# Turning image patches into token columns: 14-row sets, flattened patches and whole transposes

## The chip, the cores and the metric

The kernel runs on one core of one Trainium2 chip. The metric is the device time of one execution in microseconds (us), and the number that counts is the median over several runs. A profiled execution has a time of its own.

## The reference

Four RGB images of 224 x 224 go through a small vision tower of two layers. The change is in the first step alone, the tokenizer: each image is cut into 28 x 28 patches of 8 x 8 pixels in 3 channels, the 192 numbers of a patch are normalised, multiplied by W1, normalised again, and sent through a small network. Attention and a mixture of experts follow, twice, in layers that the change leaves alone.

```python
patches = x.reshape(b, c, hp, P, wp, P)                     # b=4, c=3, hp=wp=28, P=8
patches = jnp.transpose(patches, (0, 2, 4, 3, 5, 1))
patches = patches.reshape(b, hp * wp, P * P * c)            # 4 x 784 x 192
tokens = layernorm(patches, ln1_g, ln1_b)
tokens = tokens @ W1 + b1                                   # 192 -> 256
tokens = layernorm(tokens, ln2_g, ln2_b)
tokens = jnp.concatenate([tokens, tokens, tokens], axis=1)  # three equal copies
h1 = silu(layernorm(tokens @ Wp1 + bp1, lnp_g, lnp_b))
return h1 @ Wp2 + bp2
```

## The kernel before

The tokens are laid out so that TensorE can multiply them: the 192 numbers of a patch have to lie on partitions, one token per column, in the tile `pT`. The image comes from DRAM the other way round, so the front of the kernel turns it.

**Load.** The tile `img` holds one row of patches per partition: partition 28b + h is patch row h of image b (112 partitions, `QP`), and in it lie 24 pixel rows (3 channels x 8) of 224 pixels. Four DMAs fill it, one for each image, two from SP's queue and two from ScalarE's (L217). The weights W1 and Wp1 and the parameters ln1 and ln2 go ahead of them (L211 to L215). Half of ln2 comes through the queue of POOL (L111), as do b1 (L112), bp1 (L170) and the many small parameters in `stage` (L175). POOL also clears eight further rows of `img` (L168): one of them later takes the standard deviations, the rest are padding that brings a column of pixels to 32 numbers.

**Turns.** `turn_patches(k, c)` turns four patch columns (`PW`), k running over 7 groups of four and c over two halves of a patch. TensorE can take one column of pixels as a strided weight of 32 columns, so a half patch is four matmuls against the identity, each of which writes 32 partitions of the PSUM tile `ptp` (L339). A float32 matmul is recorded as two passes: 14 turns x 4 patches x 4 columns x 2 passes are the 448 records of L339. ScalarE then copies each `ptp` to `pT` (L343).

**Statistics.** `patch_stats` takes the mean and variance of each patch with 28 VectorE instructions straight from `img` (L435). `patch_stds` makes the deviations of all patches from them and has ScalarE write the square roots (L446) into a row of `img` beside the last pixels, so that the second-half turns bring the deviation into `pT` as a further input of the token matmul (`SROW` is its partition).

**Folding the weights.** `first_layers` is a generator that folds both normalisations and Wp1 into one matrix `Wall` (256 inputs with padding, 512 outputs). The permutation from the order of pixels in W1 to the order in `pT`, and the subtraction of the mean, are the matrix `perm` (L465 to L470). Its parts: transposes of ln1 and ln2 (L354, L357), the bias matmul (L374), W1 through `perm` (L390, L394), the bias through Wp1 (L397), then transposes of `Wall` (L404), the product with Wp1 (L412), and the last VectorE steps (L417 to L428).

**Order.** All of this stands in one block whose order on VectorE, TensorE and ScalarE is written by hand (`tc.manual_schedule`): each of these engines works through its instructions in the order of the Python code. The block starts with 16 warm-up transposes on TensorE (L479) and ends with a transpose of `stage` (L504) and its copy to `cols` (L505, called `turned`). Outside of the block, the loads of the later weights wait for the first statistics (`arrived[0]`), and the zero fill of the DRAM tables `xrows` and `yrows` (L536) waits for `turned`.

**After it.** `first_steps` multiplies 128 tokens at a time with `Wall` (L601), in 25 tiles; `pL` collects the tokens that are left over of each image (L577). `transposed` (L267) is the helper with which the rest of the kernel turns 128 x 128 blocks. Everything behind the tokenizer is the same in both versions.

Of the kernel before, what the change touches and what calls it, by code (L numbers as in the profile page):

```python
# [21 lines left out]
F32 = mybir.dt.float32  # L22
I32 = mybir.dt.int32
AF = mybir.ActivationFunctionType
ALU = mybir.AluOpType
# [9 lines left out]
NT = NI * TPI + 1  # L35
LT = NT - 1
QP = NI * HP
TOK = NI * SEQ
REP = 3
D = 256  # L40
# [28 lines left out]
def tile_vit_tower(ctx: ExitStack, tc: tile.TileContext, a: dict, out: bass.AP):  # L69
# [10 lines left out]
    def ps_tile(name):  # L80
        return psum.tile([P, 512], F32, tag="ps", name=name)
# [82 lines left out]
    nrows = sum(k for _, k, _ in plan)  # L164
    WID = HP * PATCH
    CY = CH * PATCH
    img = tokp.tile([QP, 32, WID], F32, tag="img", name="img")
    nc.gpsimd.memset(img[:, CY:, :], 0.0)  # L168
    bp1 = tokp.tile([TT, D], F32, tag="bp1", name="bp1")
    nc.gpsimd.dma_start(out=bp1, in_=a["L0_tok_bp1"].partition_broadcast(TT))  # L170
    stage = const.tile([nrows, P], F32, tag="stage", name="stage")
# [36 lines left out]
    attr = attention.enter_context(tc.tile_pool(name="attr", bufs=2, side="right"))  # L208
    front = ctx.enter_context(ExitStack())
    tokw = front.enter_context(tc.tile_pool(name="tokw", bufs=2, side="right"))  # L210
    nc.sync.dma_start(out=W1, in_=a["L0_tok_W1"].rearrange("(s p) n -> p s n", p=KP))  # L211
    nc.scalar.dma_start(out=Wp1, in_=a["L0_tok_Wp1"].rearrange("(c p) n -> p c n", p=P))
    nc.sync.dma_start(out=ln1[:1], in_=a["L0_tok_ln1_g"].unsqueeze(0))
    nc.scalar.dma_start(out=ln2[:2], in_=a["L0_tok_ln2_g"].rearrange("(r p) -> r p", p=P))
    nc.sync.dma_start(out=ln1[1:], in_=a["L0_tok_ln1_b"].unsqueeze(0))  # L215
    for b, eng in ((0, nc.sync), (3, nc.scalar), (1, nc.sync), (2, nc.scalar)):
        eng.dma_start(  # L217
            out=img[b * HP : (b + 1) * HP, :CY, :].rearrange("h (c p) w -> h c (p w)", c=CH),
            in_=a["x"][b].rearrange("c (h p) w -> h c (p w)", p=PATCH),
        )  # L220


# [109 lines left out]
    SROW = 3 * 32 + CY  # L332

    def turn_patches(k, c):
        pt = ps_tile("ptp")
        for j in range(PW):
            x0 = (k * PW + j) * PATCH + 4 * c
            for g in range(4):
                nc.tensor.matmul(  # L339
                    pt[32 * g : 32 * (g + 1), j * QP : (j + 1) * QP], img[:, :, x0 + g],  # L340
                    ident[:QP, :QP], start=True, stop=True,
                )
        nc.scalar.copy(  # L343
            pT[:, c, :, k * PW : (k + 1) * PW],
            pt[:, : PW * QP].rearrange("p (w q) -> p q w", w=PW),
        )

    def first_layers():
# [39 lines left out]
        for i in range(2):  # L388
            for half in range(2):
                nc.tensor.matmul(  # L390
                    pp[:, i, :], perm[:, half, i].rearrange("p g k -> p (g k)"),
                    W1g[:, half, :], start=(half == 0), stop=(half == 1 and i == 0),
                )
        nc.tensor.matmul(pp[:, 1, :], srow, b1, start=False, stop=True)  # L394
# [37 lines left out]

    def patch_stats(k):
        for w in range(k * PW, (k + 1) * PW):
            got = nc.vector.bn_stats(pst[:, w, :], img[:, :CY, w * PATCH : (w + 1) * PATCH])  # L435
            arrived.append(got.ins.name)

    def patch_stds(k0, k1):
        w0, n = k0 * PW, (k1 - k0) * PW
        st, v = pst[:, w0 : w0 + n], pv[:, w0 : w0 + n]  # L440
        d = tokp.tile([QP, HP], F32, tag="pd", name="pd", bufs=2)[:, :n]
# [12 lines left out]
    perm = tokp.tile([KP, 2, 2, 4, 32], F32, tag="perm", name="perm")  # L454
    srow = tokp.tile([1, P], F32, tag="srow", name="srow")
    pst = tokp.tile([QP, HP, 6], F32, tag="pst", name="pst")
    pv = tokp.tile([QP, HP], F32, tag="pv", name="pv")
    root_ = tokp.tile([1, 1], F32, tag="root", name="root")
    one_ = ones[:1]
    ENG = mybir.EngineType  # L460
# [1 line left out]
    with tc.manual_schedule(engines=by_hand):  # L462
        nc.vector.memset(srow, 0.0)
        nc.vector.memset(srow[:, SROW : SROW + 1], 1.0)
        nc.vector.memset(perm, 0.0)  # L465
        nc.vector.memset(perm[:, :, :, :, :CY], -1.0 / PD)
        by_x = ident[:KP, :KP].rearrange("p (y x c) -> p x c y", x=PATCH, c=CH)
        for half in range(2):
            for i in range(2):
                nc.vector.tensor_scalar(  # L470
                    perm[:, half, i, :, :CY].rearrange("p g (c y) -> p g c y", c=CH)[
                        :, :, :, 4 * half : 4 * (half + 1)
                    ],
                    by_x[:, 4 * i : 4 * (i + 1)], -1.0 / PD, None, ALU.add,
                )
        nc.scalar.activation(root_, one_, AF.Sqrt, bias=one_)
        warm = ps_tile("pwarm")
        for _ in range(16):
            nc.tensor.transpose(warm[:, :P], ident, ident)  # L479
# [24 lines left out]
        nc.tensor.transpose(pc[:, :nrows], stage, ident[:nrows, :nrows])  # L504
        turned = nc.vector.tensor_copy(cols, pc[:, :nrows])  # L505
# [70 lines left out]
    for c in range(2):  # L576
        nc.vector.tensor_copy(pL[:, c, :, :LEFT], left(pTf[:, c, :]))  # L577

    def pixels(c, t):
        if t == LT:  # L580
            return pL[:, c].rearrange("p b n -> p (b n)")
        n0 = t // TPI * SEQ + t % TPI * TT
        return pTf[:, c, n0 : n0 + TT]

# [6 lines left out]
    def first_steps(g):  # L591

        tiles = turns[g]
        n = len(tiles)
        y = tokp.tile([TT, GT, D], F32, tag="y", name="y", bufs=2)
        st = small.tile([TT, GT, 6], F32, tag="st", name="st")
        mv = small.tile([TT, GT, 2], F32, tag="mv", name="mv")
        for j in range(n):
            pm = ps_tile("pw1")[:TT]
            for c in range(2):  # L600
                nc.tensor.matmul(  # L601
                    pm, pixels(c, tiles[j]), Wall[:, c, :], start=(c == 0), stop=(c == 1)
                )
# [27 lines left out]
        normed[g] = xn  # L631
# [1754 lines left out]
```

## Time and profile before

| | us |
|---|---|
| median of 3 runs | 777.82 (776.65 to 778.97) |
| profiled execution, its own time | 778.21 |
| its span in the profile | 776.5 |
| images landed | 16.74 after the start of the span |
| first turn on TensorE (L339) | 16.88 |
| first token matmul (L601) | 33.13 |

The profile names engines PE (TensorE matmuls), PEld (its weight loads), DVE (VectorE), ACT (ScalarE), POOL (GpSimd) and SP. A line of a timeline gives start, length, engine, source line, instruction, tiles (written <- read), shapes and count; in square brackets stands how long the engine was idle before it and what ended that. A line of the groups gives the busy time, the mean of one in ns, and idle time before them. Matmuls are pipelined, so that the start-to-start distance and not the recorded length of one tells what it costs. The mean granted TensorE clock in the profiled execution is 0.964 of full speed.

### The profile page before, as it was taken

The numbers are of one execution on the slowest core, as the hardware profiler recorded it, in microseconds if no ns is written. First come the engines' busy times: TensorE is split into PE (matmuls) and PEld (weight loads), VectorE is DVE, ScalarE is ACT, GpSimd is POOL, SyncE is SP. The second block draws the span as 40 slices with busy tenths as digits, with TensorE's granted clock in tenths as the row PEclk, the third lists the DMA queues.
The fourth block names the chain that finished last, engine by engine and source line by source line (L and its number), as shares of the span: only waits on it lengthen the run. The fifth ranks groups of instructions, "written<-read, shape, count | busy, mean of one in ns | idle before, by whom it ended". The sixth has DMA issues, their size and how long they took to land.

```text
span 776.5 us, 10602 instructions
## 1 busy us (share of the span) xinstructions
PE 706.8 (91%) x3407; PEld 484.9 (62%) x3407; DVE 472.9 (61%) x1486; ACT 330.9 (43%) x790; POOL 125.3 (16%) x233
## 2 busy tenths in 40 slices
PE   7989899999977887888899998669999999999997
PEld 5736555566654665777788884537776775554653
DVE  5476785769996643456444767348986845444441
ACT  1465775556683641342222326325445522222221
POOL 6300000000064234400003035715000000000000
PEclk9999999999997878999999999879999999999999
DMA  6699998000012922432324352302000013323333
GB/s 167 193 425 423 426 424 341 1 1 0 1 70 77 375 102 95 130 101 69 89 89 127 104 155 72 98 24 72 12 0 1 5 27 89 91 62 96 105 111 108
DMA packets 56175, 96.24 MB, mean 124 GB/s; under 512 B 6434, under 2 KB 46088, under 8 KB 56120
## 3 DMA queue, kind: packets, MB, share of 16 engines
q1 hardware_dynamic: 49648, 79.38, 28.8%
q0 software_dynamic: 5600, 14.32, 6.1%
q10 hardware_dynamic: 872, 1.86, 0.8%
q8 instruction: 27, 0.44, 0.2%
q14 instruction: 28, 0.23, 0.1%
HBM read 30.45 MB, written 65.09 MB: 123 GB/s over the span
## 4 chain that ended last, share of the span: by engine, by line
PE 68%; DVE 17%; ACT 6%; issue 2%; another core or an unknown queue 2%; DMA 2%; DVEq 1%; ACTq 0%
PE pb L1461 12%; PE pe L276 6%; PE pyb L1479 5%; PE pqk L1927 5%; PE ps L276 4%; PE pt L267 4%; PE pkv L276 4%; PE pw L601 3%; PE pwp L287 3%; PE ps L2336 3%; DVE oT L909 3%; PE pout L2106 2%; PE pout L2111 2%; PE pukx L2026 2%
## 5 line engine op out<-in xcount | busy, mean ns | idle before, releaser
L1100 POOL DMA_INDIRECT xrows<-xn,pos x50 | 52.9, 1058 | 249.5 <-DVE nm L959 190.2
L1684 POOL DMA_INDIRECT ys<-yrows,pos x50 | 48.4, 968 | 160.3 <-DMA yrows<-yb 124.8
L1461 PE MATMUL pb<-xTb,own 128*128 128x256 f32 (+1 forms) x240 | 56.5, 381 | 8.8 <-DVE own L1437 6.3
L1467 ACT ACTIVATE hb<-pb,own 128x256 f32<-128x256 f32 (+1 forms) x74 | 33.5, 457 | 67.0 <-PE pb L1461 52.1
L1927 PE MATMUL pqk<-Wqkv,lxT 128*128 128x512 f32 x100 | 48.8, 636 | 12.8 <-ACT lxT L90 12.8
L1479 PE MATMUL pyb<-own,hb 128*128 128x256 f32 x216 | 53.2, 387 | 1.8 <-ACT hb L1467 1.0
L1461 PEld LDWEIGHTS pb<-xTb,own 128*128 128x128 f32 x240 | 42.8, 200 | 17.4 <-ACT hb L1467 6.9
L1461 PE MATMUL pb<-hb,own 128*128 128x256 f32 (+1 forms) x240 | 52.4, 360 | 1.3 <-issue 0.7
L1485 DVE TENSOR_TENSOR yb<-pyb,eb 128x512 f32<-128x512 f32 (+1 forms) x30 | 19.1, 637 | 44.9 <-PE pyb L1479 33.7
L1479 PEld LDWEIGHTS pyb<-own,hb 128*128 128x128 f32 x216 | 41.0, 194 | 8.5 <-ACT hb L1467 1.8
L276 PE MATMUL pe<-xT,eW 128*128 128x512 f32 (+1 forms) x112 | 46.0, 553 | 0.0
L1461 PEld LDWEIGHTS pb<-hb,own 128*128 128x128 f32 x240 | 40.5, 191 | 6.5 <-issue 1.9
L601 PE MATMUL pw<-Wall,pT 128*128 128x512 f32 x96 | 42.6, 593 | 0.0
L267 PE MATMUL pt<-ident,xn 128*128 128x128 f32 x200 | 31.9, 292 | 11.4 <-DVE xn L627 6.6
L1450 ACT COPY xTb<-ptb 128x512 f32<-128x512 f32 (+1 forms) x30 | 16.2, 540 | 58.8 <-PE ptb L1446 48.5
L267 PEld LDWEIGHTS pt<-ident,xn 128*128 128x128 f32 x200 | 24.9, 148 | 26.3 <-issue 8.2
L1927 PEld LDWEIGHTS pqk<-Wqkv,lxT 128*128 128x128 f32 x100 | 19.9, 206 | 34.2 <-issue 18.8
L1469 DVE TENSOR_SCALAR hb<-pb,own 128x256 f32<-128x256 f32 (+1 forms) x46 | 20.5, 445 | 29.6 <-PE pb L1461 19.8
L863 DVE SCALAR_TENSOR_TENSOR prod<-kq 128x784 f32<-128x784 f32 x32 | 30.5, 970 | 6.1 <-ACT kq L1277 3.4
L276 PEld LDWEIGHTS pe<-xT,eW 128*128 128x128 f32 x112 | 20.2, 190 | 21.6 <-issue 16.5
L1437 DVE COPY own<-ew 128x1540 f32 x30 | 28.8, 962 | 6.3 <-ACT xTb L1450 1.9
L1941 ACT ACTIVATE qk<-qk 128x256 f32<-128x256 f32 x50 | 20.4, 408 | 25.1 <-DVE qk L1933 22.3
(418 smaller groups left out, 1466.2 us busy)
## 6 DMA issues: line engine op xcount, KB each, us to landing
xrows<-nothing SPq DMA_DIRECT2D x22, 896.0 KB
yrows<-nothing SPq DMA_DIRECT2D x22, 896.0 KB
out_dram<-h SPq DMA_DIRECT2D x23, 384.0 KB
xb<-xrows SPq DMA_DIRECT2D x24, 256.0 KB
yrows<-yb SPq DMA_DIRECT2D x24, 256.0 KB
ew<-in_L_ffn_expert_w_dram SPq DMA_DIRECT2D x6, 768.0 KB
wb<-wd SPq DMA_DIRECT2D x16, 128.0 KB
img<-in_x_dram SPq DMA_DIRECT2D x2, 588.0 KB
```

Of the source, the lines that this page charges most:

```text
L267: nc.tensor.transpose(pt[:, j * TT : (j + 1) * TT], xn[:, j, c * P : (c + 1) * P], ident[:TT, :TT])
L276: nc.tensor.matmul(pm[: wcols.stop - wcols.start, :n], w[:, c, wcols], xT(c), start=(c == 0), stop=(c == chunks - 1),)
L287: nc.tensor.matmul(pm[:, i, :], xT(c, t), w[:, c, :], start=(c == 0), stop=(c == chunks - 1))
L601: nc.tensor.matmul(pm, pixels(c, tiles[j]), Wall[:, c, :], start=(c == 0), stop=(c == 1))
L863: nc.vector.scalar_tensor_tensor(prod, qTs[s][:, o, :], 1.0, kT[:, o, t * SEQ : (t + 1) * SEQ], ALU.mult, ALU.mult, accum_out=atts[s][:, o ...
L1100: put = nc.gpsimd.indirect_dma_start(out=xrows[:, :], out_offset=bass.IndirectOffsetOnAxis(ap=pos[:, k, t0 + j : t0 + j + 1], axis=0), in_ ...
L1437: nc.vector.tensor_copy(w, ewf[0][:, bass.ds(off, EW)])
L1461: nc.tensor.matmul(pm, wm[:, c, o * P : (o + 1) * P], src[:, c, :], start=(c == 0), stop=(c == 1),)
L1467: nc.scalar.activation(dst[:, o, :], pm, AF.Relu, bias=b)
L1479: nc.tensor.matmul(pm[:, t, :], src[:, c, t * P : (t + 1) * P], wm[:, c, :], start=(c == 0), stop=(c == 1),)
L1684: got = nc.gpsimd.indirect_dma_start(out=y[:, j, k, :], out_offset=None, in_=yrows[:, :], in_offset=bass.IndirectOffsetOnAxis(ap=pos[:, k, ...
L1927: nc.tensor.matmul(pqk, xTs[u][:, c, cut(j, 1)], Wqkv[:, c, : 2 * D], start=(c == 0), stop=(c == 1),)
```

## The change

The images are loaded in sets of 14 patch rows, half an image each. Set o goes to partitions o, o + 9, o + 18, ..., so that eight sets fill places 0 to 7 of each nine; a ninth transfer reads set 0 again into place 8, whose results are not used. That makes 126 partitions (`IP`) and nine DMAs, five on SP's queue and four on ScalarE's, and the small parameters go ahead of W1 and Wp1.

A new step `flatten` copies four patches so that a patch's 192 numbers lie side by side, followed by one place for the deviation; the copies live in `flat`, which borrows the space of the later tile `vT`. Two of the seven run on VectorE and five on ScalarE. `turn_patches` then transposes a patch of all 126 rows whole, in two chunks of 128 and 65 columns: 14 turns x 4 patches = 56 transposes. ScalarE's copy out of PSUM puts rows and sets in order and drops the ninth; the last one goes to VectorE. The padding of `img` and its memset go, the warm-up is 6 transposes instead of 16, `perm` is built in one step per half, and the order written by hand is new. `K1` holds the two chunk heights for the matmuls that read `pT`.

```diff
+HH = HP // 2
+SETS = 2 * NI
+PITCH = SETS + 1
+IP = HH * PITCH
...
-    img = tokp.tile([QP, 32, WID], F32, tag="img", name="img")
-    nc.gpsimd.memset(img[:, CY:, :], 0.0)
+    img = tokp.tile([IP, CY, WID], F32, tag="img", name="img")
...
-    nc.sync.dma_start(out=W1, in_=a["L0_tok_W1"].rearrange("(s p) n -> p s n", p=KP))
-    nc.scalar.dma_start(out=Wp1, in_=a["L0_tok_Wp1"].rearrange("(c p) n -> p c n", p=P))
     nc.sync.dma_start(out=ln1[:1], in_=a["L0_tok_ln1_g"].unsqueeze(0))
     nc.scalar.dma_start(out=ln2[:2], in_=a["L0_tok_ln2_g"].rearrange("(r p) -> r p", p=P))
     nc.sync.dma_start(out=ln1[1:], in_=a["L0_tok_ln1_b"].unsqueeze(0))
-    for b, eng in ((0, nc.sync), (3, nc.scalar), (1, nc.sync), (2, nc.scalar)):
-        eng.dma_start(
-            out=img[b * HP : (b + 1) * HP, :CY, :].rearrange("h (c p) w -> h c (p w)", c=CH),
-            in_=a["x"][b].rearrange("c (h p) w -> h c (p w)", p=PATCH),
+    nc.sync.dma_start(out=W1, in_=a["L0_tok_W1"].rearrange("(s p) n -> p s n", p=KP))
+    nc.scalar.dma_start(out=Wp1, in_=a["L0_tok_Wp1"].rearrange("(c p) n -> p c n", p=P))
+    for o in range(PITCH):
+        b, i = divmod(o % SETS, 2)
+        (nc.scalar if o % 2 else nc.sync).dma_start(
+            out=img[o::PITCH].rearrange("h (c p) w -> h c (p w)", c=CH),
+            in_=a["x"][b].rearrange("c (i h p) w -> i h c (p w)", i=2, p=PATCH)[i],
         )
...
+    SROW = PD - P
+    K1 = (P, SROW + 1)
+    NPX = PD + 1
+    flat = vT.rearrange("p c n -> p (c n)")[:IP, : HP * NPX].rearrange("q (w f) -> q w f", f=NPX)
+
+    def flatten(k, put):
+        put(
+            flat[:, k * PW : (k + 1) * PW, :PD].rearrange("q w (y x) -> q w y x", x=PATCH),
+            img[:, :, k * PW * PATCH : (k + 1) * PW * PATCH].rearrange(
+                "q y (w x) -> q w y x", x=PATCH
+            ),
+        )
+
+    def turn_patches(k, c, put=nc.scalar.copy):
+        pt, n = ps_tile("ptp"), K1[c]
         for j in range(PW):
-            x0 = (k * PW + j) * PATCH + 4 * c
-            for g in range(4):
-                nc.tensor.matmul(
-                    pt[32 * g : 32 * (g + 1), j * QP : (j + 1) * QP], img[:, :, x0 + g],
-                    ident[:QP, :QP], start=True, stop=True,
-                )
-        nc.scalar.copy(
-            pT[:, c, :, k * PW : (k + 1) * PW],
-            pt[:, : PW * QP].rearrange("p (w q) -> p q w", w=PW),
+            nc.tensor.transpose(
+                pt[:n, j * IP : (j + 1) * IP], flat[:, k * PW + j, c * P : c * P + n],
+                ident[:IP, :IP],
+            )
+        put(
+            pT[:n, c, :, k * PW : (k + 1) * PW].rearrange("p (o h) w -> p o h w", o=SETS),
+            pt[:n, : PW * IP].rearrange("p (w h o) -> p o h w", w=PW, h=HH)[:, :SETS],
         )
...
         nc.scalar.activation(
-            img[:, CY, w0 * PATCH : (w0 + n) * PATCH].rearrange("q (w x) -> q w x", x=PATCH)[
-                :, :, PATCH - 1
-            ],
-            v, AF.Sqrt, bias=eps[:QP], scale=1.0 / PD,
+            flat[:, w0 : w0 + n, PD], v, AF.Sqrt, bias=eps[:IP], scale=1.0 / PD,
         )
...
-        for _ in range(16):
+        for _ in range(6):
             nc.tensor.transpose(warm[:, :P], ident, ident)
         steps = first_layers()
         next(steps)
         NK = HP // PW
         cut0 = 5
-        for k in range(3):
-            turn_patches(k, 0)
-        for k in range(cut0):
+        flatten(0, nc.vector.tensor_copy)
+        flatten(1, nc.scalar.copy)
+        turn_patches(0, 0)
+        for k in range(2):
             patch_stats(k)
+        flatten(3, nc.vector.tensor_copy)
+        flatten(2, nc.scalar.copy)
+        turn_patches(1, 0)
         next(steps)
-        for k in range(3, cut0):
-            turn_patches(k, 0)
+        for k in range(2, cut0):
+            patch_stats(k)
+        turn_patches(2, 0)
+        flatten(4, nc.scalar.copy)
         next(steps)
-        for k in range(cut0, NK):
-            turn_patches(k, 0)
+        turn_patches(3, 0)
+        flatten(5, nc.scalar.copy)
+        turn_patches(4, 0)
         patch_stds(0, cut0)
+        turn_patches(5, 0)
+        flatten(6, nc.scalar.copy)
+        for k in range(2):
+            turn_patches(k, 1)
+        turn_patches(6, 0)
         for k in range(cut0, NK):
             patch_stats(k)
-        for k in range(cut0 - 1):
+        for k in range(2, cut0):
             turn_patches(k, 1)
         patch_stds(cut0, NK)
-        for k in range(cut0 - 1, NK):
-            turn_patches(k, 1)
         next(steps)
+        turn_patches(5, 1)
+        turn_patches(6, 1, nc.vector.tensor_copy)
```

More of the change, by code (lines that the diff above doesn't have):

```diff
@@ L331, in tile_vit_tower @@
     nc.gpsimd.memset(pL, 1.0)
-    SROW = 3 * 32 + CY
-    def turn_patches(k, c):
-        pt = ps_tile("ptp")
-        for j in range(PW):
-            x0 = (k * PW + j) * PATCH + 4 * c
-            for g in range(4):
-                nc.tensor.matmul(
-                    pt[32 * g : 32 * (g + 1), j * QP : (j + 1) * QP], img[:, :, x0 + g],
-                    ident[:QP, :QP], start=True, stop=True,
-                )
-        nc.scalar.copy(
-            pT[:, c, :, k * PW : (k + 1) * PW],
-            pt[:, : PW * QP].rearrange("p (w q) -> p q w", w=PW),
+    SROW = PD - P
[11 more added lines that the diff above has]
+        pt, n = ps_tile("ptp"), K1[c]
+        for j in range(PW):
+            nc.tensor.transpose(
[5 more added lines that the diff above has]
+            pt[:n, : PW * IP].rearrange("p (w h o) -> p o h w", w=PW, h=HH)[:, :SETS],
         )
@@ L390, in first_layers @@
                 nc.tensor.matmul(
-                    pp[:, i, :], perm[:, half, i].rearrange("p g k -> p (g k)"),
+                    pp[:, i, :], perm[:, half, i * P : (i + 1) * P],
                     W1g[:, half, :], start=(half == 0), stop=(half == 1 and i == 0),
@@ L434, in patch_stats @@
         for w in range(k * PW, (k + 1) * PW):
-            got = nc.vector.bn_stats(pst[:, w, :], img[:, :CY, w * PATCH : (w + 1) * PATCH])
+            got = nc.vector.bn_stats(pst[:, w, :], img[:, :, w * PATCH : (w + 1) * PATCH])
             arrived.append(got.ins.name)
@@ L440, in patch_stds @@
         st, v = pst[:, w0 : w0 + n], pv[:, w0 : w0 + n]
-        d = tokp.tile([QP, HP], F32, tag="pd", name="pd", bufs=2)[:, :n]
+        d = tokp.tile([IP, HP], F32, tag="pd", name="pd", bufs=2)[:, :n]
         nc.vector.tensor_tensor(d, st[:, :, 1], st[:, :, 4], ALU.subtract)
@@ L446, in patch_stds @@
         nc.scalar.activation(
-            img[:, CY, w0 * PATCH : (w0 + n) * PATCH].rearrange("q (w x) -> q w x", x=PATCH)[
-                :, :, PATCH - 1
-            ],
-            v, AF.Sqrt, bias=eps[:QP], scale=1.0 / PD,
+            flat[:, w0 : w0 + n, PD], v, AF.Sqrt, bias=eps[:IP], scale=1.0 / PD,
         )
     Wall = tokp.tile([P, 2, 2 * D], F32, tag="Wall", name="Wall")
-    perm = tokp.tile([KP, 2, 2, 4, 32], F32, tag="perm", name="perm")
+    perm = tokp.tile([KP, 2, 2 * P], F32, tag="perm", name="perm")
     srow = tokp.tile([1, P], F32, tag="srow", name="srow")
-    pst = tokp.tile([QP, HP, 6], F32, tag="pst", name="pst")
-    pv = tokp.tile([QP, HP], F32, tag="pv", name="pv")
+    pst = tokp.tile([IP, HP, 6], F32, tag="pst", name="pst")
+    pv = tokp.tile([IP, HP], F32, tag="pv", name="pv")
     root_ = tokp.tile([1, 1], F32, tag="root", name="root")
@@ L465, in tile_vit_tower @@
         nc.vector.memset(perm, 0.0)
-        nc.vector.memset(perm[:, :, :, :, :CY], -1.0 / PD)
-        by_x = ident[:KP, :KP].rearrange("p (y x c) -> p x c y", x=PATCH, c=CH)
+        nc.vector.memset(perm[:, :, :PD], -1.0 / PD)
+        by_y = ident[:KP, :KP].rearrange("p (y x c) -> p c y x", x=PATCH, c=CH)
         for half in range(2):
[L469 to L475, printed above, removed]
+            nc.vector.tensor_scalar(
+                perm[:, half, :PD].rearrange("p (c y x) -> p c y x", c=CH, x=PATCH)[
+                    :, :, 4 * half : 4 * (half + 1)
+                ],
+                by_y, -1.0 / PD, None, ALU.add,
+            )
         nc.scalar.activation(root_, one_, AF.Sqrt, bias=one_)
         warm = ps_tile("pwarm")
-        for _ in range(16):
+        for _ in range(6):
             nc.tensor.transpose(warm[:, :P], ident, ident)
@@ L575, in tile_vit_tower @@
     pTf = pT.rearrange("p c q w -> p c (q w)")
-    for c in range(2):
-        nc.vector.tensor_copy(pL[:, c, :, :LEFT], left(pTf[:, c, :]))
+    for c, n in enumerate(K1):
+        nc.vector.tensor_copy(pL[:n, c, :, :LEFT], left(pTf[:n, c, :]))
     def pixels(c, t):
         if t == LT:
-            return pL[:, c].rearrange("p b n -> p (b n)")
+            return pL[: K1[c], c].rearrange("p b n -> p (b n)")
         n0 = t // TPI * SEQ + t % TPI * TT
-        return pTf[:, c, n0 : n0 + TT]
+        return pTf[: K1[c], c, n0 : n0 + TT]
     def first_rows(g):
@@ L601, in first_steps @@
                 nc.tensor.matmul(
-                    pm, pixels(c, tiles[j]), Wall[:, c, :], start=(c == 0), stop=(c == 1)
+                    pm, pixels(c, tiles[j]), Wall[: K1[c], c, :], start=(c == 0), stop=(c == 1)
                 )
```

## The prediction

> **What bounds the kernel now.** First the busy shares on the page: TensorE works in 91% of the span, so a microsecond comes off the end only if TensorE's own stream gets shorter or starts earlier.
>
> ```profile
> PE 706.8 (91%) x3407; PEld 484.9 (62%) x3407; DVE 472.9 (61%) x1486; ACT 330.9 (43%) x790; POOL 125.3 (16%) x233
> ```
>
> Next the chain that ended last, cut to the first 90 us (start, length, what):
>
> ```profile
> 2.31 14.44 DMA img<-in_x_dram
> 16.74 0.14 issue
> 16.88 3.04 PE ptp L339 x96
> ...
> 20.50 1.74 PE ptp L339 x64
> ...
> 24.16 1.77 PE ptp L339 x58
> ...
> 26.76 4.09 PE ptp L339 x160
> ...
> 33.01 0.19 PE pc L504
> 33.20 7.08 PE pw L601 x16
> ```
>
> The end hangs on the image load until 16.74, then on the 448 passes of turn_patches until 33.01; at 33.20 the token matmuls (L601) start, and from there the chain is almost all TensorE and its feeders. Their start is what I forecast: every microsecond it moves should reach the end, since the next late thing, the zero fill of xrows and yrows, is released by `turned`, just after L504, and moves along; the weights wait for the first bn_stats, which moves too.
>
> Third, the timeline of that stretch (start, length, engine, instruction, [idle before]):
>
> ```profile
> 2.59 3.67 PE L479 MATMUL pwarm<-ident 128*128 128x128 f32 x16 [2.59 <-POOL ident masks.py:199]
> 7.10 0.26 PE L357 MATMUL pgb<-ident,ln 4*128 4x4 f32 x1 [0.59 <-DMA ln<-in_L_tok_ln_b_dram]
> 14.27 2.07 PE L397 MATMUL pbw<-Wp,bb 128*128 128x256 f32 x4
> 71.41 1.04 PE L267 MATMUL pt<-ident,xn 128*128 128x128 f32 x8
> 28.55 0.54 ACT L343 COPY pT<-ptp 128x448 f32<-128x448 f32 x1 [0.23 <-PE ptp L339]
> 16.86 5.31 DVE L435 BATCH_NORM_STATS2 pst<-img 112x6 f32<-112x192 f32 x20 [1.79 <-DMA img<-in_x_dram]
> ```
>
> TensorE has a second string beside the images: folding the weights (first_layers) ends at 14.27 + 2.07 = 16.34, only 0.4 us ahead of the images. So earlier images alone buy 0.4 us on TensorE. That string starts at 7.10, when ln2's second half lands, a tiny POOL transfer issued at 1.39. ScalarE idles 0.23 us before each copy: TensorE sets the pace, one turn per 0.77 us.
>
> Last, the load's rate, from the busy time by stretches (last columns: granted clock, DMA share, GB/s):
>
> ```profile
> 10.00:12.00 2.00, 2.00 (x6) 1.64 (x5) 1.70 (x8) 0.00 (x0) 0.60 (x2) 1.00 0.89 234
> 38.00:40.00 2.00, 2.00 (x6) 0.90 (x5) 0.61 (x2) 0.37 (x1) 0.00 (x0) 1.00 0.98 412
> ```
>
> The DMA engines are about as busy during the images as in the zero fill, and move little more than half as much.
>
> [...] transposes take 3.67 / 16 = 0.23 us at first and 1.04 / 8 = 0.13 us at 71 us, and the clock column falls to 0.50 at 58.9 us after an idle 2.8 us. [...]
>
> **The change, step by step.**
>
> *Load.* W1 and Wp1 go behind three tiny loads, about 0.6 us later; their 0.45 MB then ends near 4.1 us. Nine image transfers move 9 x 14 x 3 x 7168 B = 2.71 MB instead of 2.41 (one set is read twice). Now 2.41 MB takes from 3.5 to 15.5, and landing shows 1.3 us later. At best 14 engines run at the zero fill's 412 / 16 = 25.8 GB/s each, 361 GB/s: 7.5 us. I take 7.8, so images at 4.1 + 7.8 + 1.3 = 13.2. The other bound, today's rate: 4.1 + 13 + 1.3 = 18.4, worse than now. Issues go from 4 to 9, 5 on SP and 4 on ACT, at 0.33 to 0.47 us; both queues are otherwise empty until the images land, so they are hidden, even if one waits for a semaphore as SP now does for 2.1 us. The vanished 1.60 us POOL memset of img frees `live`, for which VectorE waited until 6.5.
>
> *Weight folding.* Ten warm-up transposes go: 10 x 0.23 = 2.3 us, free only if TensorE then has ln2. I put its landing at 5.2 instead of 7.1[...]; bounds 4.4 and 7.1. The rest of the string, 9.2 us at half clock, is unchanged: it ends at 14.4 and Wall is copied by 13.1. The perm build is shorter on VectorE, well ahead of its use.
>
> *Turns.* 448 passes, 3.04 + 1.74 + 1.77 + 4.09 + 1.19 + 0.80 = 12.6 us on the chain, become 56 transposes: 7.3 us at 0.13, 12.9 at 0.23.[...]
>
> *Flattens, new.* Seven copies of 126 x 768. ScalarE copies take 0.37 us for 256 elements (L604) and 0.59 for 512 (L988), so 0.80 for 768; the bound above comes from the first row here (VectorE's from the second):
>
> ```profile
> L902 ACT ACTIVATE oT<-vT,att 128x784 f32<-128x784 f32 x5 | 4.5, 944 | 0.0
> L1437 DVE COPY own<-ew 128x1540 f32 x30 | 28.8, 962 | 6.3 <-ACT xTb L1450 1.9
> ```
>
> VectorE: 0.56[...]. Five on ScalarE are 4.0 us, two on VectorE 1.1. No flatten existed before; each stands ahead of its turn.
>
> *ScalarE becomes the pace.* 13 copies at 0.52 (0.54 alone, less overlap when back to back) = 6.8, one moved to VectorE; four of its flattens after the first copy 3.2; WcT 0.6; two square roots 0.6: 11.2 us from its first copy. That comes at 14.4 + 0.92 (four transposes at half clock) + 0.2 = 15.5. I laid the three engines' lists side by side with these durations. ScalarE then loses 2.2 us: waiting for the first turns at half clock, for the Wp1 matmuls (L412, 2.0 us of TensorE between turns 2 and 3), and for VectorE's square-root input. So its last copy ends at 28.9. The token matmuls' first half needs no second-chunk copy, as now, so they start at about 29.0; turn 6's copy on VectorE ends at 29.7, inside the 0.9 us that the first half takes. VectorE: 28 bn_stats at 0.266 = 7.4, two flattens, 1.1 of deviations, 2.0 for Wall, from 13.3: done at 24.9, hidden.
>
> *Sum.* 33.2 - 29.0 = 4.2 us, of which I take off 0.3 for semaphore hand-offs on the longer list: 3.9. The profiled execution took 778.21 (span 776.5), so 774.3; it lies 0.4 above the median of 777.82, so 773.9 to 774.3. I say **774.2**.
>
> **Rivals.**
> 1. *One of the two strings does not move.* If ln2 still lands at 7.1, folding ends at 16.3 and the same lists give 30.9: 2.3 us gained, 775.7. If the images come at 16.7, 31.8: 1.4 us, 776.6; even at 17.5, 32.2. For: the POOL landing is inferred, and reading one set twice costs bytes.[...]
> 2. *Slower: TensorE stays at half clock.*[...] All 56 transposes and the Wp1 matmuls cost double (12.9 + 3.8 us), TensorE is the bound again and L601 starts at 34.0[...]. By the lists a full clock from 21.2 on still gives 30.9, from 30 on 33.2, as now; any later is slower. For: now the clock rises only near 18 us. Against: the clock also rose at 260.3 after 2.5 us of nothing but transposes and 1 us of matmuls, so transposes count, and at half clock TensorE would be nearly always busy.
> 3. *More gain.* Full clock from 14.4, flattens at 0.75, folding done at 13.0: L601 at 27.2, 6 us, 771.8.
> 4. *The relayout is dear.* Both flatten bounds and 0.56 per copy: L601 at 29.8, 775.0; a POOL write that holds a VectorE flatten adds up to its 1.63 us (L532): 776.7.
>
> **How the numbers follow.** A measurement of this kernel tells about 0.3% (2.3 us) from no change, so faster means below 775.5. Forecast as worked: 0.46, faster. Rival 1: 0.24, of which 0.06 faster and 0.18 within the bound. Rival 3: 0.08, faster. Rival 4: 0.12, half each way. Rival 2: 0.10, slower. Faster 0.46 + 0.06 + 0.08 + 0.06 = 0.66, same 0.18 + 0.06 = 0.24, slower 0.10. The range 771.5 to 777.6 holds all but rival 2 and the tails of 1, 3 and 4.
>
> **What would show it.** Right: images landing near 13; folding's L397 ending near 14.4; transposes at 0.13 each once warm; ScalarE's idle time inside the turns gone; L601 starting at 28.5 to 30. Wrong: flattens above 1 us, L397 still ending after 16, transposes at 0.23 beyond 22 us, or an L601 that starts earlier while the end doesn't move.

## The result, and the profile after

| | before | after |
|---|---|---|
| median of 20 runs each, same chip, us | 778.12 | 773.25 |
| ratio of after to before | | 0.994 (0.9914 to 0.9965) |
| profiled execution, us; its span | 778.21; 776.5 | 774.73; 773.0 |
| images landed, us | 16.74 | 16.35 |
| folding's last bias matmul ended (L397, now L410) | 16.34 | 14.74 |
| first token matmul (L601, now L622) | 33.13 | 30.87 |

The kernel is 4.9 us faster by the medians; the forecast was 774.2. The landed time was forecast at 13.2 and the first token matmul at 29.0 to 29.3, so the sum came out close while two of its terms did not. In the fences below the lines have the numbers of the kernel after: L352 is the transposes, L342 the flattens, L356 ScalarE's copies, L425 the Wp1 matmuls, L622 the token matmuls.

TensorE's row of the busy times is as heavy a share as before, with 402 instructions fewer:

```profile
PE 702.5 (91%) x3005; PEld 479.4 (62%) x3005; DVE 475.7 (62%) x1487; ACT 333.9 (43%) x794; POOL 126.2 (16%) x232
```

The chain that ended last, first 40 us (start, length, what):

```profile
1.88 6.29 DMA img<-in_x_dram
8.18 8.17 DMA img<-in_x_dram
16.66 0.62 DVE vT L342
17.33 1.94 PE ptp L352 x8
...
20.97 2.13 PE pw L425 x8
...
23.57 0.53 ACT pT L356
24.10 0.74 ACT vT L342
...
26.84 2.06 ACT pT L356 x5
...
30.94 7.09 PE pw L622 x16
```

The chain now has two image entries: an early transfer holds the queue until 8.18, and the last transfer, issued then, lands at 8.18 + 8.17 = 16.35. In place of 448 passes on TensorE stand a flatten, a few transposes, and from 23.57 mostly ScalarE.

The timeline of the same stretch shows what TensorE and ScalarE wait for (start, length, engine, instruction, [idle before]):

```profile
5.27 0.26 PE L370 MATMUL pgb<-ident,ln 4*128 4x4 f32 x1 [0.88 <-DMA ln<-in_L_tok_ln_b_dram]
12.66 2.08 PE L410 MATMUL pbw<-Wp,bb 128*128 128x256 f32 x4
17.33 1.94 PE L352 MATMUL ptp<-ident,vT 126*128 126x126 f32 x8 [2.60 <-DVE vT L342]
20.80 2.30 PE L425 MATMUL pw<-W,WcT 128*128 128x256 f32 x8
22.94 1.02 PE L352 MATMUL ptp<-ident,vT 126*128 126x126 f32 x8
23.57 0.53 ACT L356 COPY pT<-ptp 128x448 f32<-128x448 f32 x1 [1.30 <-PE ptp L352]
```

ln2 is there at 5.27 and folding ends at 12.66 + 2.08 = 14.74, close to the forecast. But the images are not, and TensorE stands idle for 2.60 us. It comes back at half clock: eight transposes take 1.94 us (0.24 each), where eight at 22.94 take 1.02 (0.13). The clock column of the stretches stays at 1.00 there, so half clock is read from these durations, and stands below for such doubled ones. The Wp1 matmuls, partly at half clock too, stand ahead of turn 3 on TensorE, and ScalarE waits 1.30 us for that turn.

The load itself, from the busy time by stretches (length; busy us and instructions of PE, PEld, DVE, ACT, POOL; granted clock, DMA share, GB/s):

```profile
10.00:12.00 2.00, 2.00 (x5) 1.17 (x5) 0.00 (x0) 0.00 (x0) 0.00 (x0) 1.00 0.90 280
```

And the waits of SP's queue (us in total, times, longest), which issues five of the nine transfers and stops twice between them:

```profile
SPq L221 <- DMA Wp<-in_L_tok_Wp_dram: 1.2, 1, 1.2
SPq L221 <- DMA img<-in_x_dram: 1.1, 1, 1.1
```

The new layout does raise the rate, from 234 to 280 GB/s, with the engines as busy as before (0.90 against 0.89). That is 19.4 GB/s for each of 0.90 x 16 engines, not 25.8.

### The profile page after: what moved, and what is told of

It reads as the page before. It is cut to its first block, busy times and chain, and to the rows that moved or that the text cites. A ratio compares the mean times of both kernels' runs of the same rounds, so it can differ in the third digit from the quotient of the medians.

```text
span 773.0 us, 9815 instructions
## 1 busy us (share of the span) xinstructions
PE 702.5 (91%) x3005; PEld 479.4 (62%) x3005; DVE 475.7 (62%) x1487; ACT 333.9 (43%) x794; POOL 126.2 (16%) x232
## 4 chain that ended last, share of the span: by engine, by line
PE 68%; DVE 17%; ACT 7%; issue 4%; DMA 2%; DVEq 1%; another core or an unknown queue 1%; ACTq 0%
PE pb L1482 11%; PE pe L280 6%; PE pyb L1500 5%; PE ps L280 4%; PE pqk L1948 4%; PE pkv L280 4%; PE pt L271 4%; PE pw L622 3%; PE ps L2357 3%; PE pwp L291 3%; PE pukx L2047 3%; PE pout L2127 3%; DVE oT L930 3%; PE pout L2132 3%; DMA img<-in_x_dram 2%
## 5 line engine op out<-in xcount | busy, mean ns | idle before, releaser
L622 PE MATMUL pw<-Wall,pT 128*128 128x512 f32 (+1 forms) x96 | 42.7, 593 | 0.0
L1948 PEld LDWEIGHTS pqk<-Wqkv,lxT 128*128 128x128 f32 x100 | 19.9, 207 | 28.6 <-issue 26.8
L280 PEld LDWEIGHTS pe<-xT,eW 128*128 128x128 f32 x112 | 20.2, 190 | 21.6 <-issue 16.5
L1458 DVE COPY own<-ew 128x1540 f32 x30 | 28.9, 965 | 7.0 <-issue 2.6
L622 PEld LDWEIGHTS pw<-Wall,pT 128*128 128x128 f32 (+1 forms) x96 | 17.9, 189 | 20.0 <-issue 17.9
```

Of the source, the lines that this page charges most:

```text
L280: nc.tensor.matmul(pm[: wcols.stop - wcols.start, :n], w[:, c, wcols], xT(c), start=(c == 0), stop=(c == chunks - 1),)
L622: nc.tensor.matmul(pm, pixels(c, tiles[j]), Wall[: K1[c], c, :], start=(c == 0), stop=(c == 1))
L1458: nc.vector.tensor_copy(w, ewf[0][:, bass.ds(off, EW)])
L1948: nc.tensor.matmul(pqk, xTs[u][:, c, cut(j, 1)], Wqkv[:, c, : 2 * D], start=(c == 0), stop=(c == 1),)
```

## The experiments

The theory after the result: the image load still bounds the start, the shorter turns bring most of the gain, and half clock and the place of the Wp1 matmuls cost what is missing. Against it stand: the gain comes from the order of loads and the earlier folding; or from the layout of the load alone. Three sets of four ran on three chips. Before took 749.94 us in the first, 749.46 in the second and 777.47 in the third, so ratios are compared, and times inside the first 35 us, which agree between the chips (folding ends at 14.71 to 14.77 in every profile in which POOL's loads, the flattens and the 6 warm-ups are as in the kernel after and the rows lie in sets). Before itself has only the one profile above.

Two times are told for each kernel that flattens: when ScalarE's first flatten starts, which is when the images are there, and how long it is from that to the first token matmul. In the kernel after they are 16.60 and 14.27 us.

### Old transfers with the new turns

The kernel after with before's four transfers of 28 neighbouring rows.

```diff
-IP = HH * PITCH
+IP = QP
...
-            out=img[o::PITCH].rearrange("h (c p) w -> h c (p w)", c=CH),
+            out=img[b * HP : (b + 1) * HP].rearrange("h (c p) w -> h c (p w)", c=CH),
...
```

> The changed kernel with the image load of before: four transfers of 28 rows on adjacent partitions, everything else as changed. Theory A (the partitions that a transfer reaches set its rate): the load goes back to about 200 GB/s, 4.4 + 2.41 MB / 0.2 + 1.3, so the images land at 17.5 to 18 us instead of 16.35, and the token matmuls start at about 32.0 instead of 30.87; ratio to before about 0.998. Theory B (some other limit, the same for both layouts, about 280 GB/s): with 2.41 MB instead of 2.71 the images land at 14.5 to 15.3, and the token matmuls start at 29.5 to 30; ratio about 0.993.

Ratio 0.9955 (0.9927 to 0.9984). Images at 17.30, token matmuls at 32.17, 14.87 later: these times are close to Theory A's, the ratio is not (it had about 0.998). In before it is 16.27 us from the first use of the images (16.86) to the token matmuls. So the new turns are 1.4 us shorter without the new load, and the token matmuls start 0.96 us earlier although the images come late. The ratio stands for 3.4 us; what is more than the 0.96 doesn't show in the front.

### The sets alone

Before with the nine transfers and 126 rows; order of loads, warm-up and 448 passes unchanged.

```diff
-    for b, eng in ((0, nc.sync), (3, nc.scalar), (1, nc.sync), (2, nc.scalar)):
...
+    for o in range(PITCH):
...
+            out=img[o::PITCH, :CY, :].rearrange("h (c p) w -> h c (p w)", c=CH),
...
```

> The kernel before with only the nine image transfers in sets of 14 rows; its load order, 16 warm-ups, 448 passes and memset stay. Theory A: the images land earlier than 16.74, at 15.5 to 16.3. As folding the weights ends at 16.3 in any case, the turns start at most 0.4 us earlier, and with 126 rows for 112 the passes get up to an eighth longer: the token matmuls start between 32.7 and 34.3, so the ratio lies between 0.9995 and 1.0015: the sets alone bring nothing. Theory C (the earlier images are what brought the gain): they start near 31, ratio 0.997.

Ratio 0.998 (0.997 to 0.9989). The timeline of TensorE:

```profile
2.59 3.52 PE L484 MATMUL pwarm<-ident 128*128 128x128 f32 x16 [2.59 <-POOL ident masks.py:199]
...
10.80 1.13 PE L402 MATMUL pbw<-Wp,bb 128*128 128x256 f32 x4
15.48 4.51 PE L344 MATMUL ptp<-ident,img 126*32 126x126 f32 x96 [3.55 <-DMA img<-in_x_dram]
...
33.75 2.84 PE L606 MATMUL pw<-Wall,pT 128*128 128x512 f32 x6
```

The first turn starts 1.4 us earlier than in before, but after 3.55 us of idling its first 96 passes take 4.51 us where they took 3.04, and all passes are a little longer with 126 rows than with 112 (the next 64 take 1.99 us, 1.80 in before). The token matmuls start no earlier: the earlier images are spent again inside the old turns.

Two things were not expected. Folding ended at 10.80 + 1.13 = 11.93, not at 16.3: TensorE came to its full clock with the last warm-ups (16 in 3.52 us, where the same 16 took 3.67 in before), and the four bias matmuls took 1.13 us instead of 2.07. And the ratio is below 1, clear of its interval, although the token matmuls start 0.6 us later than in before. That gain of 1.5 us lies somewhere behind the front.

### Eight apart instead of nine

The kernel after with 112 partitions 8 apart and no ninth transfer.

```diff
-PITCH = SETS + 1
+PITCH = SETS
```

> The changed kernel with the sets on partitions 8 apart instead of 9: eight transfers, 112 partitions, no set read twice.[...] Theory A[...]: about 200 to 220 GB/s, so the images land at 16.7 to 17.7 us although there is 0.30 MB less to move; the token matmuls start at 31.2 to 32.2. Theory B[...]: 280 GB/s, images at 14.5 to 15.3, the token matmuls at 29.5 to 30, ratio about 0.992.

Ratio 0.999 (0.9977 to 1.0003); images at 19.13, token matmuls at 33.24, both later than either theory had them. The stretch 10 to 12 us of this kernel, then of the one with old rows:

```profile
10.00:12.00 2.00, 2.00 (x5) 1.17 (x4) 0.00 (x0) 0.00 (x0) 0.00 (x0) 1.00 0.84 195
```

```profile
10.00:12.00 2.00, 2.00 (x5) 1.00 (x3) 0.87 (x5) 0.00 (x0) 0.51 (x1) 1.00 0.92 232
```

Fewer bytes than with nine apart, and 195 instead of 280 GB/s: the rate goes with the partitions that the rows go to, and going nine apart is worth the bytes of the ninth, useless set. Being spread is not enough: 8 apart loads more slowly than side by side, 195 against 232. Why the three layouts come in this order isn't shown.

### Warmth before the first turn

```diff
         next(steps)
+        again = ps_tile("pwarm2")
+        for _ in range(10):
+            nc.tensor.transpose(again[:, :P], ident, ident)
         NK = HP // PW
```

> The changed kernel with ten more transposes of the identity on TensorE between the folding of the weights (ends at 14.7) and the first turn (17.3), where it sits idle 2.6 us. They are to end before the images are there. Theory D (the half clock until 21.7 costs time because the first turns and the Wp1 matmuls stand ahead of everything): the turns run at 0.13 us per transpose from 17.3 or soon after, and the token matmuls start at 29.7 to 30.2 instead of 30.87; ratio about 0.992 against 0.994. Theory E (ScalarE paces the turns anyway): they start at 30.5 to 30.9, no gain. The image load is the same as in the changed kernel and tells how much its landing (16.35) varies from run to run.

Ratio 0.9946 (0.9925 to 0.9967). Images at 16.42, then 13.82 us to the token matmuls at 30.24: 0.45 less than in the kernel after, and between the ranges of D and E. The first eight transposes take 1.57 us there, neither the 1.94 of half clock nor the 1.02 of full: part of them is still at half clock.

### The kernel after, again

No edit; it ran beside the next three.

> The changed kernel itself, once more, to stand beside the next three on one chip. If the front decides, its token matmuls start again near 30.9 us and its ratio to before is 0.994 to 0.996; the images land between 16.1 and 16.4 again.

Ratio 0.9959 (0.9947 to 0.9972). Images at 15.71, 0.9 us earlier than in the first profile of the same kernel and than expected, and 14.22 us to the token matmuls at 29.93, as there. The turn is steady; the landing is not.

### W1 and Wp1 first again

```diff
+    nc.sync.dma_start(out=W1, in_=a["L0_tok_W1"].rearrange("(s p) n -> p s n", p=KP))
+    nc.scalar.dma_start(out=Wp1, in_=a["L0_tok_Wp1"].rearrange("(c p) n -> p c n", p=P))
     nc.sync.dma_start(out=ln1[:1], in_=a["L0_tok_ln1_g"].unsqueeze(0))
```

> The changed kernel with W1 and Wp1 issued ahead of the three small loads again, as before the change. Theory F (the new order leaves the DMA engines without work for 0.6 us at the start, and the images bound the front, not the folding): the images land near 15.2 to 15.5 instead of 16.2, the folding ends near 15.6 instead of 14.7, the turns start near 16.2 and the token matmuls at 29.6 to 30.2: about 0.8 us less than the changed kernel, ratio lower by 0.001. Theory G (the small loads first help, since the folding starts earlier): the token matmuls start later than 30.9, or at the same time.

Ratio 0.9958 (0.9943 to 0.9974). Images at 16.95 and folding still done at 14.72: no gain. The idea that the later first packet costs 0.8 us fell.

### Wp1 matmuls behind turn 4

```diff
         turn_patches(2, 0)
         flatten(4, nc.scalar.copy)
-        next(steps)
         turn_patches(3, 0)
         flatten(5, nc.scalar.copy)
         turn_patches(4, 0)
+        next(steps)
+        flatten(6, nc.scalar.copy)
         patch_stds(0, cut0)
         turn_patches(5, 0)
-        flatten(6, nc.scalar.copy)
```

> The changed kernel with the matmuls with Wp1 (the third step of first_layers) moved behind the turns 3 and 4 in TensorE's order, and the square roots behind flatten 6 on ScalarE. Theory H (ScalarE loses 1.3 us waiting for turn 3, which stands behind these matmuls): that wait goes, the token matmuls start at 30.0 to 30.5. Theory I (the wait only moves: turn 5 then stands behind the matmuls, and the first square roots wait for a VectorE that the third flatten, 2.0 us beside POOL's writes, makes late): no gain, 30.7 to 31.

Ratio 0.9939 (0.9915 to 0.9963). From the timeline:

```profile
21.92 0.83 ACT L342 COPY vT<-img 126x768 f32<-126x768 f32 x1
22.66 0.54 ACT L356 COPY pT<-ptp 128x448 f32<-128x448 f32 x1
23.08 0.84 ACT L342 COPY vT<-img 126x768 f32<-126x768 f32 x1
23.30 1.89 PE L425 MATMUL pw<-W,WcT 128*128 128x256 f32 x8
```

Turn 3's copy (22.66) follows the flatten ahead of it with no idle time, where the kernel after waited 1.30 us. From the first flatten to the token matmuls are 13.08 us: 1.2 less. The wait was on the path, and the order by itself removes it.

### Three edits together

W1 and Wp1 first, Wp1 matmuls later, and flatten 3 in another form on VectorE.

```diff
...
-        flatten(3, nc.vector.tensor_copy)
+        flatten(3, lambda d, s: nc.vector.tensor_tensor(d, s, s, ALU.max))
...
```

> Three edits at once on the changed kernel: W1 and Wp1 first, the Wp1 matmuls behind turn 4, and flatten 3 as a maximum of a tile with itself[...]. Flatten 3 should take 0.9 to 1.0 us whatever POOL does, against 1.1 to 2.0 as a copy. If the three add up, the token matmuls start at 28.6 to 29.3 and the ratio is 0.991 to 0.993; if ScalarE is the floor whatever stands ahead of it, at 29.6 or later.

Ratio 0.9944 (0.9921 to 0.9967). Images at 17.71, 13.08 us to the token matmuls at 30.79, not 28.6 to 29.3: the same span as with the later Wp1 matmuls alone. Flatten 3 took 0.94 us here, 2.02 in the kernel after, and 0.55 to 2.16 in the other kernels that copy it; none of the difference reaches the token matmuls here.

### The order of loads and warm-up alone

Before with the small loads first and 6 warm-ups.

```diff
...
-        for _ in range(16):
+        for _ in range(6):
```

> The kernel before with only the order of the first loads and the number of warm-up transposes changed (three small loads ahead of W1 and Wp1, 6 warm-ups for 16); image rows, transfers and the 448 passes as before. Prediction's theory (the images bound the front, folding is next to them): folding ends near 14.4 to 15 instead of 16.3, but the images still land at 16.5 to 17.5, so the token matmuls start at 33.0 to 34 and the ratio to before is 0.999 to 1.002. Rival (folding is what holds the front, and the new image layout contributes little): token matmuls at 31 to 32, ratio 0.997 or less.

Ratio 1.0006 (0.9982 to 1.003). From the timeline of TensorE:

```profile
12.89 2.07 PE L397 MATMUL pbw<-Wp,bb 128*128 128x256 f32 x4
16.88 3.98 PE L339 MATMUL ptp<-ident,img 112*32 112x112 f32 x96 [1.92 <-DMA img<-in_x_dram]
...
33.70 2.84 PE L601 MATMUL pw<-Wall,pT 128*128 128x512 f32 x6
```

Folding ends at 14.96, 1.4 us earlier, and TensorE only waits 1.92 us for the images, after which its first 96 passes take 3.98 us, not 3.04. The rival that folding holds the front is out.

### Parameters behind the images

The kernel after with POOL's loads of bp1 and `stage` put into the list that waits for the first statistics.

```diff
-    nc.gpsimd.dma_start(out=bp1, in_=a["L0_tok_bp1"].partition_broadcast(TT))
...
-        nc.gpsimd.dma_start(out=stage[r0 : r0 + n, :width], in_=src)
...
+    weight_loads.append(
+        nc.gpsimd.dma_start(out=bp1, in_=a["L0_tok_bp1"].partition_broadcast(TT))
+    )
...
+        weight_loads.append(nc.gpsimd.dma_start(out=stage[r0 : r0 + n, :width], in_=src))
```

> The kernel after with POOL's loads of bp1 and of the thirteen parameter strings of stage moved behind the first bn_stats, so that nothing small shares the DMA engines with the images from about 5 us on. Theory J (small POOL packets share the engines with the image packets and hold the last of them): the stretch 6 to 12 us moves 320 GB/s or more and the images land by 15, about 1.3 us earlier than in the kernel after; token matmuls near 29, ratio to before 0.993 to 0.994. Theory K (14 partitions apart by 9 give 280 GB/s by themselves, or the issuing queues set it): 270 to 290 GB/s still, landing 15.7 to 17 as in the runs so far, ratio as the kernel after, 0.994 to 0.997.

Ratio 0.9956 (0.9931 to 0.9981). Images at 15.78, inside K's range. The 319 and 337 GB/s from 8 to 12 us are J's, the 272 from 6 to 8 are not; the last experiment decides between them. Two side effects tell more. First, POOL, no longer busy issuing, clears `nothing` early, and the timeline of POOL and VectorE shows:

```profile
5.21 1.60 POOL L555 MEMSET nothing<- 128x1792 f32 x1
...
5.59 1.47 DVE L574 TENSOR_SCALAR spare<-spare,dead 128x2 f32<-128x2 f32 x1
```

In the kernel after the same VectorE step takes 0.25 us; here it ends at 7.06, 0.25 us after POOL's write (6.81), and folding behind it ends at 16.41 instead of 14.74. The kernel of the last experiment repeats both lines, 1.60 us from 5.21 and 1.47 us from 5.59. That the write held the step is the author's reading of these times.

Second, the token matmuls start at 29.69, 1.2 us earlier than in the kernel after, but their second group of 16 starts at 62.19 against 61.98. The gain was given back in between. Stretches of the kernel after, then of this one:

```profile
54.00:56.00 2.00, 0.16 (x1) 0.18 (x1) 1.48 (x9) 1.97 (x4) 0.00 (x0) 0.90 1.06 444
...
58.00:60.00 2.00, 2.00 (x8) 1.63 (x8) 2.00 (x10) 1.98 (x3) 0.00 (x0) 0.75 1.03 434
```

```profile
54.00:56.00 2.00, 1.35 (x6) 1.13 (x7) 1.93 (x8) 1.32 (x2) 0.00 (x0) 0.50 1.01 423
...
58.00:60.00 2.00, 2.00 (x7) 1.55 (x6) 0.93 (x5) 1.19 (x2) 0.00 (x0) 0.50 0.99 416
```

The granted clock stays at 0.50 from 54 to 60 us, a longer dip, and the chain has 5.44 us for the 16 second matmuls of the tokens (L286 here) that took 4.05 (L291).

### New order and warmth together

The later Wp1 matmuls and the ten transposes in one kernel.

> The kernel after with the Wp1 matmuls behind turn 4 and flatten 6 ahead of the square roots, and ten more transposes of the identity between folding and the first turn. If the two gains are separate (the wait of ScalarE for turn 3 of 1.3 us, and turns at half clock until 21.7): 12.3 to 12.8 us from ScalarE's first flatten to the token matmuls, where the kernel after took 14.2 and each edit alone 13.1 and 13.8; ratio 0.992 to 0.994. If ScalarE's own work (11.2 us and its first flatten) is all that is left once its wait is gone, the warm-up adds nothing: 13.0 to 13.2, ratio 0.9935 to 0.995.

Ratio 0.9923 (0.9901 to 0.9945), median 771.45 beside 777.47. From the timeline of TensorE:

```profile
14.56 2.34 PE L493 MATMUL pwarm<-ident 128*128 128x128 f32 x10
17.36 1.67 PE L352 MATMUL ptp<-ident,vT 126*128 126x126 f32 x8 [0.46 <-DVE vT L342]
...
29.52 5.43 PE L625 MATMUL pw<-Wall,pT 128*128 128x512 f32 x12
```

The images come at 16.68, no earlier than in the kernel after, and 12.84 us later the token matmuls start: 1.2 us from the order, 0.2 more from the warmth, so less than two separate gains would give. Before is beaten clear of noise. Against the kernel after, the token matmuls start 1.35 us earlier, but the ratios leave it open: the kernel after had 0.994 (0.9914 to 0.9965) and 0.9959 (0.9947 to 0.9972), on other chips.

### All of it

The last two experiments in one kernel.

> The last two together: parameter loads behind the images, Wp1 matmuls later, ten transposes before the first turn. If Theory J holds: images by 15, token matmuls near 27.5 to 28, ratio 0.990 to 0.992. If Theory K holds: the same as the kernel with the new order and warm-up alone, ratio within 0.001 of it.

Ratio 0.9916 (0.9886 to 0.9947): not to be told from 0.9923. Images at 16.66. The stretch 10 to 12 us, of the kernel with parameters later and of this one, whose loads up to there are the same:

```profile
10.00:12.00 2.00, 2.00 (x6) 1.58 (x5) 1.38 (x8) 0.00 (x0) 0.52 (x3) 1.00 0.92 337
```

```profile
10.00:12.00 2.00, 2.00 (x6) 1.57 (x5) 1.40 (x8) 0.00 (x0) 0.53 (x3) 1.00 0.89 251
```

337 in one execution and 251 in the other, images at 15.78 and 16.66: POOL's small loads don't explain the landing. With them it was 15.71, 16.42, 16.60, 16.68 and 17.14. The packet records of these five traces show where the spread arises: nine tenths of the images' 7 KB packets had ended by 13.71 to 14.35 us, the last one at 14.95, 15.68, 15.68, 15.97 and 16.43, in the same order. In all ten profiles of sets 9 apart the last six packets are those of SP's queue, which has five of the nine transfers. Why they lag stays open; no kernel here shares the transfers out differently.

## Why the prediction was right, and where it was wrong

**The load** is the step that failed: "At best 14 engines run at the zero fill's 412 / 16 = 25.8 GB/s each, 361 GB/s". The 14 can be read from before's packet records: from 6 to 13 us mostly 14 image packets were under way at once, in the zero fill 16. The engines were as busy as assumed, but moved 19.4 GB/s each. In the packet records a 7 KB packet of the zero fill took 0.272 us; those of the images, from 6 to 13 us, took 0.335 on average, where they took 0.437 in before and 0.508 with sets 8 apart. They ran from 4.13 to 15.68, 11.6 us instead of 7.8: nine tenths had ended by 13.78, the last came singly. The landing showed 0.7 us after the last one, not 1.3: 16.35 instead of 13.2. SP's queue from 15 to 15.8 us (packets, MB, share of 16 engines):

```profile
q1 hardware_dynamic: 3, 0.01, 4.6%
```

Rows sent 9 apart are better than neighbouring ones (with the small loads first, flattens started at 17.30 in one execution with old rows, and at 15.71 to 17.14 in five with the sets), but their packets take longer than the zero fill's. That image packets would move at the zero fill's pace in the new layout was the author's estimate; no row of before showed it. The bound at today's rate should have been 18.9 instead of 18.4, since at 2.41 MB in 12 us the 2.71 MB take 13.5 us, not 13. The issues, costed as hidden at 0.33 to 0.47 us, took 3.52 / 4 = 0.88 each on ScalarE's queue, and SP's were spread until 8.99; whether that delays the landing wasn't separated.

```profile
1.88 3.52 ACTq L221 DMA_DIRECT2D img<-in_x_dram  x4
```

**Folding**: ln2 at 5.2 and the end at 14.4 were forecast, 5.27 and 14.74 measured. The 5.2 was the author's estimate, and why ln2 came 1.8 us earlier isn't shown. Right, and worth nothing by itself, as the prediction said of the one string without the other and the kernel with only the new order shows.

**The clock**: half was expected for the first turns only, with TensorE going from folding straight into them; when full would come was the author's estimate. With the images late it idled 2.60 us and ran at half clock until about 21.6 (two records of the Wp1 matmuls in each 0.4 us before, three and four after). Where it did go straight on, with the parameters later (turns at 16.46 behind a folding that ended at 16.41), the first eight transposes took 1.94 us as well, and the Wp1 matmuls at 19.93 were at full clock (eight in 1.99 us, as in before). Rival 2 was built on half clock, but it did not last so long that TensorE became the bound; the warmth is worth 0.45 us on its own and 0.2 beside the new order.

**ScalarE's pace** was right in kind and somewhat too slow in size. The forecast had 13.4 us from its first copy to the end of its last (15.5 to 28.9), 11.2 of work and 2.2 of waits. Measured are 12.4 (18.47 to 30.89): 10.1 of work and 0.25 + 1.30 + 0.73 = 2.3 of waits, the longest one for the turn behind the Wp1 matmuls. Flattens cost 0.83 and, back to back, 0.73 to 0.74 (0.80 assumed); copies back to back 2.68 / 6 = 0.45 (0.52 assumed). VectorE's second flatten, then the last lines of ScalarE:

```profile
19.27 2.02 DVE L342 COPY vT<-img 126x768 f32<-126x768 f32 x1
...
26.73 2.68 ACT L356 COPY pT<-ptp 65x448 f32<-65x448 f32 x6
29.30 0.33 ACT L459 ACTIVATE vT<-pv,eps 126x8 f32<-126x8 f32 x1
30.36 0.53 ACT L356 COPY pT<-ptp 65x448 f32<-65x448 f32 x1 [0.73 <-PE ptp L352]
```

The VectorE flattens cost 0.61 (0.56 assumed, an estimate of the author's) in the first and 2.02 in the second. The POOL write that Rival 4 named had ended at 19.05, and POOL went on with many small ones; where its clearing was done early, with the parameters later, this flatten took 0.55 and 0.56. So a flatten was slowed as in Rival 4, and that POOL's writes did it is the author's reading of these times; but it had time to spare. The one hand-off from the landing (16.35) to the first flatten (16.66) took as much as the whole term of 0.3 us.

**The sum.** What happened is nearest to Rival 1, images that don't move; its 31.8 for images at 16.7 was too late, in part because of ScalarE's pace. The token matmuls began 2.26 us earlier in the first pair of profiles and 3.2 in the repetition, instead of 3.9. The prediction had 3.5 of its 4.2 us from the load and 0.7 from the turns; the pair shows 0.4 from the load and 1.9 from the turns.

**From there to the end** the prediction let the gain through unchanged. The spans show 1.24 us more gained behind the first token matmul (743.37 to 742.13), 0.47 of it up to the second group (31.51 to 31.04). It isn't explained, and single executions can't explain it: on the third chip, where before takes about as long as here (777.47), the four profiles have 735.6 to 744.6 from the first token matmul to the end, over the same instructions. Part of that spread is the clock dip near 56 us, which took 1.4 us back where parameters came later. The old rows and the sets alone show the same gap: by the ratio they gain 2.4 and 2.1 us more than the start of their token matmuls does, against the one profile of before. So 774.2 met 773.25 with a front 1.6 us short, and with 1.24 us behind it and a median that moved 4.9 us where the profiled pair moved 3.5. None of that was in the forecast, and that the number was met so closely is luck.

## What to carry to other kernels

A transfer's rate is to be taken from a row with the same shape of packets and partitions, not from the fastest row of the page: rows nine partitions apart raised 234 to 280 GB/s, not to 361. A load is there only with its slowest packets: nine tenths of this one had ended 1.9 us before the last. When one of two strings into a stage is shortened, work out what the engine does in the gap: here it idled 2.60 us, and ten transposes put there were worth 0.45 us. And where an in-order engine feeds the engine that sets the pace, moving a block that nobody needs yet (eight matmuls, 2 us) behind the next feeds was worth 1.2 us, half of what the first pair of profiles shows for the whole front.

## What the runs showed of the hardware that was not expected

- Image transfers with rows 9 apart took 0.88 us each to issue on ScalarE's queue (and so did rows 8 apart), against 0.44 for rows side by side in before.
- Rows 8 apart loaded at 195 GB/s, more slowly than neighbouring rows at 232.
- The same loads were first used between 15.71 and 17.14 us in different executions, with no difference in the program ahead of them; the last few packets, all of one queue, made the difference.
- The same 16 warm-up transposes brought TensorE to its full clock in one execution (3.52 us, with the sets alone; the bias matmuls after them took 1.13 us) and not in another (3.67 us, before; 2.07 us).
- Beside an early POOL write of 1.60 us, in two executions, a VectorE instruction of two elements a row took 1.47 us and ended 0.25 us after the write; without it, in the kernel after, it took 0.25.
- In one execution an earlier start was lost at a later dip of the TensorE clock: 1.2 us gained at 30 us were gone at 62.
